# GpSimd in place of VectorE for two elementwise steps of an attention stage: the output bias on the residual tile, and the scale and shift of the turned x

## The chip, the cores and the metric

The kernel runs on one core of one Trainium2 chip. The metric is the device time of one execution in microseconds (us), the median of several runs. The core has a matrix engine (TensorE, PE in the profile; its weight loads are PEld), three engines for elementwise work (VectorE or DVE, ScalarE or ACT, GpSimd or POOL), and SyncE (SP), which here only issues DMAs. Each engine works through its own queue of instructions in the order of the program and waits on semaphores where it needs another's result. DMAs are issued from the queues of SP, ACT and POOL.

## The reference

A transformer-like block on x of shape (8, 512, 1024), float32, in four stages, each with its own layer norm:

```python
x = x + attn_a(_layernorm(x))   # 32 heads of 32, softmax, then ctx @ ow + ob
x = x + ffn(_layernorm(x))      # dense 1024x1024, rows and tokens gated by clusters
x = x + attn_b(_layernorm(x))   # 4 heads of 256, causal sigmoid attention
x = x + ffn(_layernorm(x))
```

The change is in the first line alone. Its layer norm is `(x - m) / sqrt(v + eps)`; its last step is

```python
qkv = x @ attn_qkvw + attn_qkvb
...
return ctx @ attn_ow + attn_ob
```

so that the residual tile gets x + attn_ob + ctx @ attn_ow.

## The kernel before

The 4096 tokens are 8 batches of 512, and 32 tiles of 128 tokens (`NTILE`). The 32 heads are 8 groups of four (`GH`), so the first stage has 64 units: unit n is group g = n % 8 of batch b = n // 8. The first stage takes the span up to about 2530 us; the two dense stages and the sigmoid attention follow.

A unit (the long loop over `n` in `softmax_attention`) has four rounds i = 0 to 3. In a round TensorE computes the scores of unit n+1 by rows (`rows_step`: 16 matmuls, L905, into the one buffer `sc` in PSUM), VectorE takes the negated row maxima from them (L906, out `nmax`), TensorE computes the scores of unit n again by keys into the same buffer `sc` (`keys_step`, L934 and L937), and ScalarE takes the exponential (L939, out `pT`). Between these stand pieces of other work for TensorE, dealt out by `filler`: the projections of unit n+2 (L578, `qk` and `v`), and the output products of the batch before. The one buffer makes a ring: L934 cannot begin before L906 has read `sc`.

The exponentials of the four key tiles are added up: the first two by GpSimd in two halves (L948 in `sum_step`), the third and the fourth by VectorE (L950). The sum ends in the denominators (L973, `normalize`).

When a unit's four maxima are there, `split_max` (called at the end of the unit, for unit n+1) cuts them into three bfloat16 parts with five small VectorE instructions in a row, L912 to L916, on 128 x 16 elements; L913 and L915 are subtractions of two tiles in SBUF. In the first round of the next unit, between its L906 and its L934, TensorE turns these parts (`turn_max`, out `tpm`, line L578 by its helper `product`) for use by L934.

The normalised and turned x of batch b+1 is prepared while batch b runs (`norm_tasks(b + 1)`). x arrives already turned from DRAM (`turned`, L535, tile `xT`); the mean and the root of each token are computed from the straight x (`stats`, `root`, `shift`), sent to DRAM as two rows (`send`, L550) and read back to all partitions (`spread`, L554, tile `rows`). `apply(k, j)` then multiplies a quarter of `xT` (128 x 1024 elements) by the roots (k = 0) or adds the shifts (k = 1) in place, line L558. There are 8 such instructions a batch, for batches 1 to 7: 56. `norm_tasks` lists them for the groups after the one with `spread`: idle, idle and three of them, idle, idle and three more, idle, idle and the last two. These lists go into the deque `side`, which is dealt out over the five calls of `between` in a unit. The Strassen-like sums of the quarters of `xT` (`left_tasks`, L991 and L1377) follow in group 6, and the products of the next batch read those.

The output projection runs over pairs of tiles (`out_pair`), two pairs a batch. `load(m)` brings x's tile into `r` (L766), `bias(m)` adds the broadcast bias `ob_s` in place (L769, 128 x 1024 elements), and `done(k)` adds the products as they end (L788). Of a pair, `bias(0)` is put behind the last product of the pair before, `bias(1)` ahead of the fourth of the seven products; the fourth is the first to add into `r[1]`. `leave(m)` writes the finished tile to DRAM from GpSimd's queue (L816). There are 32 bias instructions; in the last pair the tile is named `spare`, and the lists of the last two pairs run alone, behind the last unit.

GpSimd has, besides L948, the roots (`rstd`, L249, a power on 128 x 1 to 128 x 4 elements) and its DMA issues.

## Time and profile before

| | |
|---|---|
| runs | 3715.86 us median of 3 (3714.45 to 3716.66) |
| span of the profiled execution | 3715.1 us |
| VectorE busy | 2539.7 us, 68% of the span |
| ScalarE busy | 927.8 us, 25% |
| GpSimd busy | 594.9 us, 16% |
| TensorE clock granted | 0.999 of full speed |
| L906 row maxima, VectorE | 256 of 2.289 us each |
| L950 sums, VectorE | 128 of 2.281 us each |
| L249 roots `ln_rstd`, GpSimd | 64 of 0.586 us each |
| L816 write of `r`, issued by GpSimd | 30 of 512 KB, 4.5 us to landing |

A row of the profile names line, engine, operation, what is written from what (`out<-in`, buffer numbers left out), shapes, how many, the busy time in us, the mean of one in ns, and the idle time of the engine just before them with what ended it. A timeline row begins with the start in us and the time taken. The 40 digits in "busy tenths" are shares of equal slices of the span. In lists of waits the last number is the longest single wait.

### The profile page before, as it was taken

The page shows a single profiled execution, that of the slowest core. Times are in us where ns is not written, and L with a number is a line of the kernel's source. Part 1 is how long each engine was busy: PE and PEld are TensorE (multiplying, and loading weights), DVE is VectorE, ACT ScalarE, POOL GpSimd, SP SyncE. Part 2 cuts the span into 40 slices and gives each one's busy share as a digit, 9 for nine tenths or more (in the row PEclk, how much of TensorE's full clock was granted, in tenths as well). Part 3 has the DMA queues.
Part 4 walks back from the last instruction along what each step waited for, and adds up shares of the span by engine and source line. Part 5 has one row for each costly group of instructions (what it writes and reads, how often), then busy time and mean ns, then how long its engine had stood idle before and what let it go on. Part 6 is the DMA issues. An engine that isn't in the chain of part 4 may idle for free.

```text
span 3715.1 us, 76365 instructions
## 1 busy us (share of the span) xinstructions
PE 3677.4 (99%) x32792; PEld 1876.7 (51%) x32792; DVE 2539.7 (68%) x3497; ACT 927.8 (25%) x1017; POOL 594.9 (16%) x574
## 2 busy tenths in 40 slices
PE   8999999999999999999999999999999999999999
PEld 4444544544545455445445445444444467774444
DVE  4777676767667677766767767666788845556656
ACT  1222222222222222222222222222111144430000
POOL 1222111111111111111111111111000044530000
PEclk9999999999999999999999999999999999999999
DMA  5335444645655555465465454347566767763332
GB/s 184 113 122 179 142 143 147 192 138 157 185 153 150 159 162 163 133 198 152 139 182 159 143 150 124 122 156 244 158 180 179 184 186 234 222 220 127 133 132 98
DMA packets 728641, 598.55 MB, mean 161 GB/s; under 512 B 322152, under 2 KB 574064, under 8 KB 728304
## 3 DMA queue, kind: packets, MB, share of 16 engines
q1 hardware_dynamic: 701072, 496.40, 46.6%
q0 software_dynamic: 22912, 81.54, 5.7%
q10 hardware_dynamic: 4320, 15.73, 1.0%
q8 instruction: 259, 4.24, 0.5%
q14 instruction: 78, 0.64, 0.0%
HBM read 459.30 MB, written 134.25 MB: 160 GB/s over the span
## 4 chain that ended last, share of the span: by engine, by line
PE 95%; DVE 3%; DMA 1%; issue 1%; ACT 0%; POOL 0%; SPq 0%; DVEq 0%; ACTq 0%; POOLq 0%
PE mm L578 42%; PE dense L1285 20%; PE sc L905 7%; PE av L961 6%; PE sc L937 6%; PE csc L1347 4%; PE o L1366 4%; PE sc L934 2%; PE logitsT L339 1%; PE den L973 1%; PE tp L291 1%; DVE nmax L906 1%; DVE sum L950 1%; PE tpm L578 0%; DVE s L1377 0%
## 5 line engine op out<-in xcount | busy, mean ns | idle before, releaser
L906 DVE TENSOR_REDUCE nmax<-sc 128x4 f32<-128x2048 f32 x256 | 586.0, 2289 | 295.3 <-PE sc L905 295.2
L939 ACT ACTIVATE pT<-sc 128x2048 f32<-128x2048 f32 x256 | 480.8, 1878 | 1122.3 <-PE sc L937 1122.3
L948 POOL TENSOR_TENSOR sum<-pT,pT 128x1024 f32<-128x1024 f32 x128 | 309.4, 2438 | 750.0 <-ACT pT L939 678.1
L578 PE MATMUL mm<-xT,w 128*64 128x256 f32 (+1 forms) x3736 | 428.1, 383 | 0.0
L578 PEld LDWEIGHTS mm<-xT,w 128*64 128x64 f32 (+1 forms) x3736 | 241.5, 135 | 204.1 <-issue 54.3
L578 PE MATMUL mm<-s,w 128*32 128x256 f32 (+1 forms) x3672 | 321.2, 381 | 1.2 <-DVE qk L158 1.2
L950 DVE TENSOR_TENSOR sum<-sum,pT 128x2048 f32<-128x2048 f32 x128 | 292.0, 2281 | 0.9 <-ACT pT L939 0.9
L905 PE MATMUL sc<-qk,qk 32*64 32x512 f32 x4096 | 285.1, 613 | 0.5 <-ACT pT L939 0.4
L156 DVE TENSOR_TENSOR u<-dense,u 128x512 f32<-128x512 f32 x223 | 148.0, 685 | 184.7 <-PE dense L1285 169.3
L578 PEld LDWEIGHTS mm<-s,w 128*32 128x32 f32 (+1 forms) x3672 | 180.4, 122 | 180.4 <-issue 68.9
L937 PE MATMUL sc<-qk,qk 32*128 32x512 f32 x2048 | 263.7, 589 | 0.0
L578 PE MATMUL mm<-ow,ctxT 128*32 128x512 f32 (+2 forms) x1276 | 247.2, 599 | 3.0 <-DMA ow<-o_T 2.8
L961 PE MATMUL av<-pT,v 128*32 128x512 f32 x2048 | 246.4, 598 | 0.2 <-ACT pT L939 0.2
L1285 PE MATMUL dense<-sum,s 128*128 128x512 f32 x512 | 231.8, 593 | 0.0
L578 PEld LDWEIGHTS mm<-w,xT 128*64 128x64 f32 (+1 forms) x3888 | 197.5, 133 | 62.2 <-issue 48.9
L578 PE MATMUL mm<-w,xT 128*64 128x128 f32 (+1 forms) x3888 | 218.1, 274 | 0.0
L158 DVE SCALAR_TENSOR_TENSOR qk<-mm,qkvb_s,qk 128x256 f32<-128x256 f32 x224 | 107.6, 480 | 123.2 <-PE mm L578 119.2
L1285 PE MATMUL dense<-wT_s,dT_b 128*128 128x512 f32 x384 | 171.2, 593 | 0.0
L1285 PE MATMUL dense<-wT_s,dT_a 128*128 128x512 f32 x384 | 171.2, 593 | 0.0
L578 PE MATMUL mm<-ow,c 128*64 128x512 f32 (+2 forms) x864 | 169.9, 596 | 0.2 <-DMA ow<-in_ow 0.2
L578 PE MATMUL mm<-w,s 128*64 128x128 f32 x2688 | 162.5, 274 | 0.0
L578 PEld LDWEIGHTS mm<-w,s 128*64 128x64 f32 x2688 | 148.0, 137 | 22.9 <-issue 22.9
(236 smaller groups left out, 4468.8 us busy)
## 6 DMA issues: line engine op xcount, KB each, us to landing
w<-in_qkvw SPq DMA_DIRECT2D x252, 256.0 KB, 3.0
ow<-o_T SPq DMA_DIRECT2D x240, 256.0 KB, 3.6
w<-qk_T SPq DMA_DIRECT2D x224, 256.0 KB, 2.8
ow<-in_ow SPq DMA_DIRECT2D x180, 256.0 KB, 3.3
w<-v_T SPq DMA_DIRECT2D x112, 256.0 KB, 2.7
x<-in_x SPq DMA_DIRECT2D x32, 512.0 KB, 5.3
dT_a<-xT SPq DMA_DIRECT2D x32, 512.0 KB, 5.7
x_a<-x SPq DMA_DIRECT2D x32, 512.0 KB, 6.5
```

Of the source, the lines that this page charges most:

```text
L156: nc.vector.tensor_tensor(out, acc, other, ALU.add)
L578: nc.tensor.matmul(out[cols], lhsT[:, cols], rhs, **flags)
L905: nc.tensor.matmul(sc[ts(j, P // 2), h, :], st["q"][rows, cols], st["k"][rows, :], start=True, stop=True)
L906: nc.vector.tensor_reduce(st["nmax"][:, qt, :], sc, AX.X, ALU.max, negate=True)
L937: nc.tensor.matmul(sc[:, h, :], st["k"][rows, ts(kt, P)], st["q"][rows, :], start=False, stop=True)
L939: nc.scalar.activation(pT, sc, AF.Exp, scale=SCALE_A)
L948: nc.gpsimd.tensor_tensor(st["sum"][:, h, :], st["pT", 0][:, h, :], st["pT", 1][:, h, :], ALU.add)
L950: nc.vector.tensor_tensor(st["sum"], st["sum"], st["pT", kt], ALU.add)
L961: nc.tensor.matmul(st["av"][rows, :], st["v"][:, kt, rows], pT[:, h, :], start=(kt == 0), stop=(kt == TPB - 1))
L1285: nc.tensor.matmul(st["acc"], st["left"][LEFT[k]][:, c, :], self.w[RIGHT[k]][:, c, :], start=(c == 0), stop=(c == half - 1),)
L1347: nc.tensor.matmul(sc[:, AT_OFF[i] : AT_OFF[i] + n], k[:, c, ts(i, P)], xT[:, c, i * P :], start=(c == 0), stop=(c == 1),)
L1366: nc.tensor.matmul(acc[:, j - jj, :], at[:, start : start + P], self.v[b * TPB + i][:, cols], start=(i == 0), stop=(i == j),)
```

## The change

Two calls move from VectorE's queue to GpSimd's. Operands, shapes, the place in the program and the arithmetic stay as they are.

```diff
         def apply(k, j):
             part, rows = xT[:, ts(j, 2), :], st["all"][:, k, :].unsqueeze(1).to_broadcast([P, 2, S])
-            nc.vector.tensor_tensor(part, part, rows, (ALU.mult, ALU.add)[k])
+            nc.gpsimd.tensor_tensor(part, part, rows, (ALU.mult, ALU.add)[k])
...
         def bias(m):
-            nc.vector.tensor_tensor(r[m], r[m], ob_s, ALU.add)
+            nc.gpsimd.tensor_tensor(r[m], r[m], ob_s, ALU.add)
```

The queues of TensorE, ScalarE and SyncE keep their instructions and their order; where one of them waited for one of these 88 instructions it now waits for GpSimd. VectorE's queue loses the 88. GpSimd's queue gets them at the places that the program's order gives. For the x of each of the batches 3 to 7 that order is:

```
L948 sum x2
L769 r
L558 xT x3
L816 write of r
L948 sum x2
L249 ln_rstd
L558 xT
L948 sum x2
L558 xT
L816 write of r
L769 r
L558 xT
L249 ln_rstd
L558 xT
L948 sum x2
L558 xT
L948 sum x2
L769 r
```

For batch 2 the first group has one L558 instead of three; for batch 1 the groups are three, three and two, each behind a unit's L948.

## The prediction

> **What bounds the kernel now.** I read the page's first part, then the waits of TensorE in the attention stage (83 to 2530 us, where all 88 moved instructions but the last four lie), then the groups of the moved lines, then timelines.

> ```profile
> PE 3677.4 (99%) x32792; PEld 1876.7 (51%) x32792; DVE 2539.7 (68%) x3497; ACT 927.8 (25%) x1017; POOL 594.9 (16%) x574
> ```

> ```profile
> PE sc L934 <- DVE nmax L906: 4.7, 5, 2.3
> PE den L973 <- DVE sum L950: 1.4, 1, 1.4
> PE mm L578 <- DVE qk L158: 1.2, 6, 0.2
> PE tpm L578 <- DVE parts L916: 1.0, 1, 1.0
> ```

> TensorE is busy 99% of the span; in the stage's 2447.0 us it is busy 2435.9, so 11.1 us is all that any relief of other engines could give there. VectorE is late for it a dozen times only. But lateness is near everywhere: the timelines below show how little room VectorE has at one place.

> **The change part by part.** The groups:

> ```profile
> L558 DVE TENSOR_TENSOR xT<-xT,rows 128x1024 f32<-128x1024 f32 x56 | 73.1, 1308 | 0.2
> L769 DVE TENSOR_TENSOR r<-r,ob_s 128x1024 f32<-128x1024 f32 x30 | 36.5, 1216 | 0.0
> L948 POOL TENSOR_TENSOR sum<-pT,pT 128x1024 f32<-128x1024 f32 x128 | 309.4, 2438 | 750.0 <-ACT pT L939 678.1 <-ACT lg_a L350 40.3 <-DVE c L785 31.6
> ```

> *Removed from VectorE:* 73.1 + 36.5 + 2 x 1.2 = 112 us. On TensorE's time I give this 0: none of the waits above follows a moved instruction in one busy run of VectorE; at the 2.3 us wait, VectorE had last sat idle for TensorE behind its two L558. The bounds are 0 and a gain of 11.1 us.

> *Added to GpSimd:* GpSimd does not run these two forms now. The nearest row is L948, same shape, 2.41 us at the median; another add-like form (L1333, 128 x 1024) takes 2.34, and the largest L948 2.89. I take 2.41: 88 x 2.41 = 212 us on an engine that is idle 84% of the span. So the question is only what becomes late.

> *The bias.* L769 waits for its load and for what stands ahead of it on GpSimd. I put each one behind the end of GpSimd's previous instruction in the trace and added 2.41 us. The consumer L788 then still begins 3.2 us later at the tightest place before the last two pairs, mostly 4.2 us (L948 ends at 1234.55, bias to 1237.0, L788 at 1241.3). Cost 0; were GpSimd slower by more than that 3.2 us, each of some 14 such places would hold VectorE. Behind the bias on GpSimd's queue stand L816's writes, put off by up to 0.5 us; the tiles they write are read in the dense stage, and `r` has three buffers.

> In the last two pairs the queue is tight. At 2528.5 the root L249 would run, the bias follow to about 2531.5, and L788, which began at 2529.63, be 1.9 us late; L261 behind it would wait for the second bias, to 2533.9, and ScalarE's L254 start 2.5 us later than at 2531.62. Its 1.24 us end at 2535.3, ahead of the transposes at 2537.07. Cost between 0 and 1.9 us; I take 1.0.

> *The scale and shift.* The quarter is read by L991 and L1377 a unit later: at least 10 us of room. The instructions queued behind L558 on GpSimd (L948, L249, L816) are put off by at most 0.5 us in this placing. What decides is another thing: the two engines already exclude each other in this trace.

> ```profile
> 519.68 4.79 POOL L948 TENSOR_TENSOR sum<-pT,pT 128x1024 f32<-128x1024 f32 x2 [9.27 <-ACT pT L939]
> 523.62 1.93 DVE L558 TENSOR_TENSOR xT<-xT,rows 128x1024 f32<-128x1024 f32 x1
> L394 DVE TENSOR_TENSOR hits_b<-hits_b,some x7: 226/1290/1314, 3131.9 to 3349.7; 128x64 f32<-128x64 f32 x7
> ```

> (Rows with "x7:" give the count, the shortest, median and longest in ns, the first and last start.) L558 begins under L948, which ends at 524.47, and takes 1.93 us instead of 1.22: its last 1.09 us lie behind that end. So do all seven L558 that meet L948, and L394 of only 128 x 64 elements, 1.29 us instead of 0.22, under GpSimd's L1333. Row maxima L906 (one input, in PSUM) run under L948 at their usual 2.29. So a VectorE instruction with two inputs in SBUF waits for the end of the GpSimd instruction. In the one case with two L948 in a row (2362.7 us, L785 of 2.93 instead of 0.69), VectorE ran between the two and the second took 2.89: they take turns.

> Now the place. For batches 3 to 7 three L558 stand together behind a bias on GpSimd's queue and wait for the DMA `rows`:

> ```profile
> L554 SPq DMA_DIRECT2D rows<-rows x7: 343/422/1022, 168.8 to 2030.1; - x7
> DMA to landing us min/median/max: 5.0/5.2/5.5
> 1399.19 0.42 SPq L554 DMA_DIRECT2D rows<-rows  x1
> 1403.84 2.28 DVE L950 TENSOR_TENSOR sum<-sum,pT 128x2048 f32<-128x2048 f32 x1
> 1408.60 0.20 DVE L912 CAST parts<-nmax 128x16 bf16<-128x16 f32 x1
> 1408.83 0.18 DVE L913 TENSOR_TENSOR rest<-nmax,parts 128x16 f32<-128x16 f32 x1
> 1409.28 0.18 DVE L915 TENSOR_TENSOR rest<-rest,parts 128x16 f32<-128x16 f32 x1
> 1409.50 0.20 DVE L916 CAST parts<-rest 128x16 bf16<-128x16 f32 x1
> 1409.59 2.29 DVE L906 TENSOR_REDUCE nmax<-sc 128x4 f32<-128x2048 f32 x1
> ```

> ```profile
> 1408.14 1.11 PE L905 MATMUL sc<-qk,qk 32*64 32x512 f32 x16
> 1410.96 0.39 PE L578 MATMUL tpm<-ident_h,parts 128*64 128x128 bf16 x8
> 1413.01 0.39 PE L934 MATMUL sc<-shift,ones_h 32*128 32x512 bf16 x4
> ```

> `rows` lands at 1404.17, 0.3 us into VectorE's L950, which has two inputs in SBUF and ends at 1406.12. GpSimd's first L558 therefore runs from there to about 1408.4, the second to 1410.85. VectorE comes to L913 at 1408.83: it waits until 1410.85. L914 follows, and L915 asks at 1411.2, when the third L558 has begun; it waits until 1413.3. L916 ends at 1413.6 instead of 1409.70, and L906 at 1415.8 instead of 1411.88. TensorE's `tpm` had 1.26 us of room behind L916, L934 1.13 us behind L906. Both are used up: L934 begins at 1415.85 instead of 1413.01, 2.9 us late on the engine that bounds. The other four batches have the same rows: L554 at 768.44, 1083.65, 1714.60 and 2030.06, landing 5.0 to 5.5 us later, 0.3 to 0.8 us into an L950. For batch 2 (landing 458.39) one L558 ends at 462.5, ahead of L913 at 462.96: nothing. Batch 1's bursts meet no instruction of this kind.

> Bounds of this term: if GpSimd needs over 0.4 us between one L558 and the next, which waits for it, L913 slips through, L915 alone waits until 1411.4, and 0.9 us is paid; if such small instructions are not held at all, 0. If GpSimd's form takes 2.89 us, as the longest L948, each of the two waits grows by 0.5: 3.9 us. I take 2.9, as the held rows are nearest in kind.

> Elsewhere a single L558 touches L261 and L785 at its last 0.1 to 0.3 us, before an L906 with 1.1 us of room; without that room 0.3 us each.

> [...] No run here shows a held L913 or L915 yet.

> *Sum:* 3715.1 (profiled span) + 5 x 2.9 + 1.0 (tail) - 0 = 3730.6. The median of the runs stands 0.76 above that span: 3731 us, 0.4% slower.

> **The rivals.**

> *One turn slips:* L913 gets in between two L558. 5 x 0.9 + 1.0: 3721. For it: only 0.4 us are missing. Against it: instructions of VectorE that wait for each other follow at 0.04 us (L912 to L913), and GpSimd needs ten times that.

> *The lock spares the small ones (not slower):* L913 and L915 stream through under GpSimd. It decides from where their two waits together stay under 1.13 us, the room of L934. Then 0 to 1 us remains: 3716, VectorE 112 us less busy, and no gain, as TensorE had no wait there. For it: no L913 ever met GpSimd in this trace. Against it: L394, and L248 of 128 x 4 elements that took 0.87 instead of 0.16 us under L948.

> *GpSimd is slower at these forms:* `rows` is read twice through a broadcast, which L948 does not do. Each us more costs 2 us in each of the five places, 10 in all, and from 3.2 us more the biases come late too. With 3.8 us an instruction: 3745. Against it: L1333 and L948 lie within 0.1 us.

> *Relief counts:* TensorE's matmul ends are modelled, and VectorE's delays could hide in them. At most 11.1 us: 3705. Against it: the units' lengths repeat from batch to batch with waits of 0.2 us or less.

> **How the numbers follow.** Forecast 58% (own range 3725 to 3738), one turn 11%, spared 14%, slow form 12%, relief 5%. A measurement of this kernel can tell about 0.2%, 7.4 us, from no change. Slower by more: forecast and slow form, 70%. Within: one turn and spared, 25%. Faster: relief, 5%. The range goes from 3714, just below the spared case, to 3740, the forecast with 3.3 us an instruction, and leaves out most of the slow form and the relief.

> **What would show it.** L558 and L769 on GpSimd near 2.4 us; five L913 and five L915 of about 2 us in place of 0.185; five waits of `tpm` or L934 of some 2.9 us together, each after a landing of `rows`; waits of L788 for GpSimd only behind 2528 us. I am wrong if L913 and L915 keep 0.185 us throughout, if the landing moves out of L950's time, or if waits appear in other units.

## The result, and the profile after

The changed kernel took 3735.23 us (median of 4 runs, 3733.58 to 3737.54), the kernel before 3715.36 us beside it (4 runs, 3714.45 to 3716.66): a ratio of 1.0055, 95% interval 1.0043 to 1.0067. It is some 20 us slower, more than the 0.2% that the prediction gave as the least that can be told from no change. The profiled execution after has a span of 3734.0 us, 18.9 more than before.

First the page's row of busy times, after:

```profile
PE 3682.3 (99%) x32792; PEld 1877.1 (50%) x32792; DVE 2463.6 (66%) x3409; ACT 928.0 (25%) x1017; POOL 806.2 (22%) x662
```

VectorE is busy for 76.1 us less and GpSimd for 211.3 us more, and TensorE is as full as it was. (The moved instructions were 112 us of VectorE's time; some of the others now take longer, as the rows below show, and that counts as busy.) Next, TensorE's waits in the attention stage (83 to 2550 us), after:

```profile
PE tpm L578 <- DVE parts L916: 14.9, 6, 2.9
PE sc L934 <- DVE nmax L906: 4.7, 5, 2.3
PE den L973 <- DVE sum L950: 1.4, 1, 1.4
PE mm L578 <- DVE qk L158: 1.2, 6, 0.2
```

Of the four rows that were shown of before, three stand unchanged. Only the row of `tpm` has grown, from one wait of 1.0 us to six waits of 14.9 us in all. Who was late is seen in the rows of single lines, after (count, shortest/median/longest in ns, first and last start, form):

```profile
L558 POOL TENSOR_TENSOR xT<-xT,rows x56: 2330/2362/3840, 192.8 to 2156.8; 128x1024 f32<-128x1024 f32 x56
L912 DVE CAST parts<-nmax x64: 191/194/2250, 68.1 to 2516.3; 128x16 bf16<-128x16 f32 x64
L913 DVE TENSOR_TENSOR rest<-nmax,parts x64: 184/185/2339, 68.4 to 2516.5; 128x16 f32<-128x16 f32 x64
L914 DVE CAST parts<-rest x64: 202/203/2280, 68.6 to 2516.8; 128x16 bf16<-128x16 f32 x64
L915 DVE TENSOR_TENSOR rest<-rest,parts x64: 183/185/189, 68.8 to 2517.0; 128x16 f32<-128x16 f32 x64
```

Three of the small instructions have a longest of about 2.3 us where their median is 0.2; L915 has none. The place, the preparation of batch 5, in the timeline after (start in us, time taken, in brackets the idle time ahead and what ended it):

```profile
1405.74 1.20 SPq L554 DMA_DIRECT2D rows<-rows  x1
1410.44 2.28 DVE L950 TENSOR_TENSOR sum<-sum,pT 128x2048 f32<-128x2048 f32 x1
1411.65 8.03 POOL L558 TENSOR_TENSOR xT<-xT,rows 128x1024 f32<-128x1024 f32 x3 [8.49 <-DMA rows<-rows]
1414.74 1.11 PE L905 MATMUL sc<-qk,qk 32*64 32x512 f32 x16
1415.20 2.24 DVE L912 CAST parts<-nmax 128x16 bf16<-128x16 f32 x1
1417.48 2.24 DVE L913 TENSOR_TENSOR rest<-nmax,parts 128x16 f32<-128x16 f32 x1
1419.75 0.20 DVE L914 CAST parts<-rest 128x16 bf16<-128x16 f32 x1
1419.99 0.18 DVE L915 TENSOR_TENSOR rest<-rest,parts 128x16 f32<-128x16 f32 x1
1420.21 0.20 DVE L916 CAST parts<-rest 128x16 bf16<-128x16 f32 x1
1420.30 2.28 DVE L906 TENSOR_REDUCE nmax<-sc 128x4 f32<-128x2048 f32 x1
1420.47 0.41 PE L578 MATMUL tpm<-ident_h,parts 128*64 128x128 bf16 x8 [2.73 <-DVE parts L916]
1422.64 0.39 PE L934 MATMUL sc<-shift,ones_h 32*128 32x512 bf16 x4
```

Read it from the burst. The three L558 occupy GpSimd from 1411.65 to 1419.68: the first waits for the end of L950 at 1412.72, then three of about 2.3 us follow. L912 comes at 1415.20, just after the second has begun, and ends with it at 1417.44; L913 comes at 1417.48, just after the third has begun, and ends with it at 1419.72. L914, L915 and L916 then run at their usual length. `tpm`, ready to start at 1417.74, waits 2.73 us, and L934 with it. The reduction L906 begins behind the burst, late by the two holds, and has its usual 2.28.

Where the 18.9 us are, from the starts of `tpm`, unit by unit, after minus before:

| part of the span | after minus before, us |
|---|---|
| five units with such a burst (batches 3 to 7) | 2.91 + 3.05 + 2.90 + 2.92 + 2.91 = 14.69 |
| the unit behind the burst, in two of the five places | 1.66 + 1.67 = 3.3 |
| the same unit in the other three | 0.4 together |
| last `tpm` to the end of the span | +1.5 |
| start, up to the first units | -1.2 |
| the rest | 0.2 |

The 3.3 us were not foreseen. TensorE did not wait in those two units; it ran slower. The windows, after (us; busy us and count of PE, PEld, DVE, ACT and POOL; the granted clock; DMA share; GB/s):

```profile
1098.09:1101.50 3.41, 1.06 (x16) 0.81 (x18) 3.34 (x4) 0.77 (x2) 1.78 (x1) 1.00 0.27 77
1101.50:1104.91 3.41, 3.41 (x23) 1.37 (x18) 3.41 (x3) 0.00 (x0) 0.00 (x0) 0.50 0.14 22
1736.39:1739.80 3.41, 0.77 (x14) 0.62 (x16) 3.31 (x5) 0.90 (x3) 1.84 (x1) 1.00 0.26 77
1739.80:1743.21 3.41, 3.41 (x22) 1.67 (x22) 3.41 (x2) 0.27 (x1) 0.00 (x0) 0.50 0.02 5
1418.94:1422.36 3.42, 1.89 (x24) 1.24 (x24) 3.32 (x5) 0.58 (x1) 0.74 (x1) 1.00 0.25 77
1422.36:1425.77 3.41, 3.38 (x36) 1.09 (x36) 2.81 (x3) 1.74 (x1) 0.00 (x0) 1.00 0.22 77
```

After the stalls that end at 1100.4 and about 1739 the clock granted to TensorE was 0.50 for 3.41 us, which costs half of that, 1.7 us; after the stall that ends at 1420.47 it stayed at 1.00.

### The profile page after: what moved, and what is told of

Its sections match the earlier page's. It is cut to its first block, busy times and chain, and to the rows that moved or that the text cites. A ratio compares the mean times of both kernels' runs of the same rounds, so it can differ in the third digit from the quotient of the medians.

```text
span 3734.0 us, 76377 instructions
## 1 busy us (share of the span) xinstructions
PE 3682.3 (99%) x32792; PEld 1877.1 (50%) x32792; DVE 2463.6 (66%) x3409; ACT 928.0 (25%) x1017; POOL 806.2 (22%) x662
## 4 chain that ended last, share of the span: by engine, by line
PE 93%; DVE 4%; DMA 1%; issue 1%; SPq 0%; ACT 0%; POOL 0%; DVEq 0%; ACTq 0%; POOLq 0%
PE mm L578 41%; PE dense L1285 20%; PE sc L905 7%; PE av L961 6%; PE sc L937 6%; PE o L1366 4%; PE csc L1347 4%; PE sc L934 2%; PE logitsT L339 1%; PE den L973 1%; PE tp L291 1%; DVE nmax L906 1%; DVE sum L950 1%; PE tpm L578 0%; DMA cx<-x 0%
## 5 line engine op out<-in xcount | busy, mean ns | idle before, releaser
L906 DVE TENSOR_REDUCE nmax<-sc 128x4 f32<-128x2048 f32 x256 | 586.0, 2289 | 308.2 <-PE sc L905 308.2
L939 ACT ACTIVATE pT<-sc 128x2048 f32<-128x2048 f32 x256 | 480.8, 1878 | 1127.8 <-PE sc L937 1121.7
L948 POOL TENSOR_TENSOR sum<-pT,pT 128x1024 f32<-128x1024 f32 x128 | 309.6, 2441 | 706.2 <-ACT pT L939 634.3
L578 PE MATMUL mm<-xT,w 128*64 128x256 f32 (+1 forms) x3736 | 430.0, 384 | 0.0
L578 PEld LDWEIGHTS mm<-xT,w 128*64 128x64 f32 (+1 forms) x3736 | 241.9, 135 | 204.9 <-issue 58.6
L578 PE MATMUL mm<-s,w 128*32 128x256 f32 (+1 forms) x3672 | 321.2, 381 | 1.2 <-DVE qk L158 1.2
L950 DVE TENSOR_TENSOR sum<-sum,pT 128x2048 f32<-128x2048 f32 x128 | 292.4, 2284 | 0.9 <-ACT pT L939 0.9
L905 PE MATMUL sc<-qk,qk 32*64 32x512 f32 x4096 | 285.1, 613 | 0.5 <-ACT pT L939 0.4
L578 PEld LDWEIGHTS mm<-s,w 128*32 128x32 f32 (+1 forms) x3672 | 180.4, 122 | 180.3 <-issue 68.9
L156 DVE TENSOR_TENSOR u<-dense,u 128x512 f32<-128x512 f32 x223 | 148.0, 685 | 184.9 <-PE dense L1285 169.2
L578 PE MATMUL mm<-ow,ctxT 128*32 128x512 f32 (+2 forms) x1276 | 247.4, 599 | 3.6 <-DMA ow<-o_T 3.1
L578 PEld LDWEIGHTS mm<-w,xT 128*64 128x64 f32 (+1 forms) x3888 | 197.5, 133 | 62.1 <-issue 48.9
L578 PE MATMUL mm<-w,xT 128*64 128x128 f32 (+1 forms) x3888 | 218.1, 274 | 0.0
L158 DVE SCALAR_TENSOR_TENSOR qk<-mm,qkvb_s,qk 128x256 f32<-128x256 f32 x224 | 107.5, 480 | 154.9 <-PE mm L578 152.2
L578 PE MATMUL mm<-ow,c 128*64 128x512 f32 (+2 forms) x864 | 170.2, 596 | 0.5 <-DMA ow<-o_T 0.5
L578 PE MATMUL mm<-w,s 128*64 128x128 f32 x2688 | 162.5, 274 | 0.0
L578 PEld LDWEIGHTS mm<-w,s 128*64 128x64 f32 x2688 | 148.0, 137 | 22.9 <-issue 22.9
```

The lines of the kernel that those rows point to most:

```text
L156: nc.vector.tensor_tensor(out, acc, other, ALU.add)
L578: nc.tensor.matmul(out[cols], lhsT[:, cols], rhs, **flags)
L905: nc.tensor.matmul(sc[ts(j, P // 2), h, :], st["q"][rows, cols], st["k"][rows, :], start=True, stop=True)
L906: nc.vector.tensor_reduce(st["nmax"][:, qt, :], sc, AX.X, ALU.max, negate=True)
L939: nc.scalar.activation(pT, sc, AF.Exp, scale=SCALE_A)
L948: nc.gpsimd.tensor_tensor(st["sum"][:, h, :], st["pT", 0][:, h, :], st["pT", 1][:, h, :], ALU.add)
```

## The experiments

All times are set against the kernel before on the same chip: 3714.17 us (19 runs) for the first four, 3715.19 us (33 runs) for the last four.

**The bias alone moved**

```diff
 def apply(k, j):
-    nc.gpsimd.tensor_tensor(part, part, rows, (ALU.mult, ALU.add)[k])
+    nc.vector.tensor_tensor(part, part, rows, (ALU.mult, ALU.add)[k])
```

(Diffs here are against the changed kernel.)

> Only the bias moves to GpSimd, the scale and shift stay on VectorE. Theory (three L558 together hold the small instructions of split_max): no L912 to L916 is held, all stay near 0.2 us, and only the last two pairs cost something, 1 to 1.5 us: ratio to before 1.0000 to 1.0005. Rival (every two-input instruction on GpSimd costs VectorE and so TensorE its share, wherever it stands): 32 of 88 of the 19.9 us, 7 us, ratio 1.002.

Measured: 3714.48 us, ratio 1.0001 (0.9991 to 1.0010). TensorE's waits in the stage are those of before, none of L912 to L915 is longer than usual (one L916 took 0.29 us instead of 0.20), and the bias shows in one wait of VectorE:

```profile
DVE r L788 <- POOL r L769: 3.0, 1, 3.0
```

It is the wait behind the last unit, 3.0 us long. Thirty-two instructions moved cost nothing that can be measured, which excludes the rival's 7 us.

**The scale and shift alone moved**

```diff
 def bias(m):
-    nc.gpsimd.tensor_tensor(r[m], r[m], ob_s, ALU.add)
+    nc.vector.tensor_tensor(r[m], r[m], ob_s, ALU.add)
```

> Only the scale and shift move, the bias stays on VectorE. Theory: the five waits of tpm of 2.7 to 2.9 us are there as in the changed kernel, with some drops of the granted clock behind them: 14 to 20 us, ratio 1.004 to 1.0055. Rival (every moved instruction pays alike): 56 of 88, 12.7 us, ratio 1.0034.

Measured: 3731.82 us, ratio 1.0052 (1.0035 to 1.0069). The waits of TensorE, in the same part of the span:

```profile
PE tpm L578 <- DVE parts L916: 14.7, 6, 2.8
```

The loss is here, in full as far as the intervals tell. L912 and L913 took 2.24 to 2.26 us each in all five batches.

**All moved but the three that stand together**

```diff
-    nc.gpsimd.tensor_tensor(part, part, rows, (ALU.mult, ALU.add)[k])
+    (nc.gpsimd if 2 * j + k >= 3 else nc.vector).tensor_tensor(part, part, rows, (ALU.mult, ALU.add)[k])
```

> The whole change, but the first three of the eight L558 of each batch stay on VectorE: 67 of 88 instructions are moved, and none of them stands behind the landing of rows. Theory: tpm waits 0 to 1 us in all as before, no drop of the clock behind it, only the tail's 1 to 1.5 us is left: ratio 1.0000 to 1.0005. Rival (all alike): 67 of 88 of 19.9 us, 15 us, ratio 1.004.

Measured: 3716.92 us, ratio 1.0008 (0.9998 to 1.0017). 67 of the 88 instructions run on GpSimd. The cast keeps its length throughout:

```profile
L912 DVE CAST parts<-nmax x64: 191/194/203, 69.1 to 2498.8; 128x16 bf16<-128x16 f32 x64
```

The waits of `tpm` are back at one of 1.0 us, and the units' lengths are those of before.

**Only the three that stand together moved**

```diff
-    nc.gpsimd.tensor_tensor(part, part, rows, (ALU.mult, ALU.add)[k])
+    (nc.gpsimd if 2 * j + k < 3 else nc.vector).tensor_tensor(part, part, rows, (ALU.mult, ALU.add)[k])
...
-    nc.gpsimd.tensor_tensor(r[m], r[m], ob_s, ALU.add)
+    nc.vector.tensor_tensor(r[m], r[m], ob_s, ALU.add)
```

> The reverse: only the first three L558 of each batch are on GpSimd, 21 instructions of 88. Theory: nearly the whole loss is there, five waits of tpm of 2.7 to 2.9 us plus drops of the clock, 14 to 19 us, ratio 1.004 to 1.005. Rival (all alike): 21 of 88, 4.7 us, ratio 1.0013.

Measured: 3731.20 us, ratio 1.0048 (1.0033 to 1.0063), with the waits

```profile
PE tpm L578 <- DVE parts L916: 14.7, 6, 2.8
```

Twenty-one of the 88 instructions bring the loss, and without them it goes: the two runs together show that the burst is the place.

**One of the three moved, then two**

```diff
-    nc.gpsimd.tensor_tensor(part, part, rows, (ALU.mult, ALU.add)[k])
+    (nc.gpsimd if 2 * j + k < 1 else nc.vector).tensor_tensor(part, part, rows, (ALU.mult, ALU.add)[k])
```

In the second kernel the 1 is a 2; in both the bias is on VectorE.

> Only the first L558 of each batch is on GpSimd. Theory (a held instruction waits to the end of the GpSimd instruction under way, and what counts is what is still under way when L912 comes up): the one L558 starts when L950 ends, takes 2.3 us and is over 0.2 us before L912 comes up; nothing is held, no wait of tpm beyond the 1.4 us of before: ratio 0.9995 to 1.0005. Rival (the loss goes with the number of moved instructions in the place): a third of e4's 17 us, ratio 1.0015.

> The first two L558 of each batch are on GpSimd. Theory: one of L912 and L913 is held to the end of the second, 2.2 us, five times; 1.26 us of that is covered by the room that tpm has, so five waits of tpm of 0.8 to 1.0 us, and no drop of the clock behind waits this short: 4 to 5 us, ratio 1.0010 to 1.0015. Rival (loss by the number): two thirds of e4's 17 us, ratio 1.003.

Measured: with one, 3714.12 us, ratio 0.9998 (0.9989 to 1.0007), and nothing is held:

```profile
L912 DVE CAST parts<-nmax x64: 191/194/199, 69.0 to 2499.0; 128x16 bf16<-128x16 f32 x64
```

With two, 3720.71 us, ratio 1.0016 (1.0007 to 1.0025). The same place of the second kernel in its timeline:

```profile
1405.84 2.28 DVE L950 TENSOR_TENSOR sum<-sum,pT 128x2048 f32<-128x2048 f32 x1
1406.92 5.86 POOL L558 TENSOR_TENSOR xT<-xT,rows 128x1024 f32<-128x1024 f32 x2 [12.97 <-DMA rows<-rows]
1410.60 2.24 DVE L912 CAST parts<-nmax 128x16 bf16<-128x16 f32 x1
1412.87 0.18 DVE L913 TENSOR_TENSOR rest<-nmax,parts 128x16 f32<-128x16 f32 x1
1413.81 0.41 PE L578 MATMUL tpm<-ident_h,parts 128*64 128x128 bf16 x8 [0.68 <-DVE parts L916]
```

L912 is held until the second L558 ends at 1412.78, and L913 runs freely, as there is no third. L912 is 2.05 us longer, and `tpm`'s room (1.26 us in the profile of before) covers all but 0.68 us of it; the five units are 0.85 to 0.91 us longer. So each L558 behind the first held exactly one small instruction; the first hold was covered in good part by the room, and the second, in the kernel with three, found none left. No clock drop followed these short waits.

**The rows read back earlier, the whole change otherwise kept**

```diff
-            [root, shift, send, idle, spread],
+            [root, shift, send, spread],
```

This lets `spread` be issued one call of `between` sooner, so that the burst should be over when the small instructions come.

> The whole change of 88 instructions, with the DMA of rows issued one place earlier (an idle place of the list left out), some 10 us before. Theory: the three L558 run before L950 and are over when L912 comes up; no instruction from L912 to L916 is held, no wait of tpm of over 1 us, no drop of the clock behind it; left is the tail's 1 to 1.5 us: ratio 0.9998 to 1.0008. Rival (VectorE and GpSimd share something in proportion to GpSimd's work): 1.0055 as in the changed kernel.

Measured: 3716.94 us, ratio 1.0005 (0.9996 to 1.0014). The time is back, but not by the way expected. The landing of `rows`, and the same place in the timeline:

```profile
DMA to landing us min/median/max: 7.4/8.4/9.6
1398.38 9.17 POOL L558 TENSOR_TENSOR xT<-xT,rows 128x1024 f32<-128x1024 f32 x3 [3.84 <-DMA rows<-rows]
1401.06 4.27 DVE L950 TENSOR_TENSOR sum<-sum,pT 128x2048 f32<-128x2048 f32 x1
1405.92 1.70 DVE L912 CAST parts<-nmax 128x16 bf16<-128x16 f32 x1
1408.59 0.41 PE L578 MATMUL tpm<-ident_h,parts 128*64 128x128 bf16 x8 [0.23 <-DVE parts L916]
```

The transfer took 8.4 us at the median of the three landings that this profile gives, where it took 5.2 before, and ate about half of what the earlier issue had won: in the five units L554 was issued 6.7 to 9.3 us sooner than in the changed kernel, counted from the `tpm` ahead of it, and the burst began only 3.6 to 5.2 us sooner. The burst had begun when L950 came, held it (4.27 us instead of 2.28), and ended at 1407.55, with L912 taking 1.70 us until then (1.3 to 1.7 us in the five batches). `tpm`'s room covers all but 0.23 us of this. Two holds became one short one; why the transfer took longer in that place was not tried.

**The same, and the last two pairs' bias back on VectorE**

```diff
-            [root, shift, send, idle, spread],
+            [root, shift, send, spread],
...
-            nc.gpsimd.tensor_tensor(r[m], r[m], ob_s, ALU.add)
+            (nc.gpsimd if q < 2 * (B - 1) else nc.vector).tensor_tensor(r[m], r[m], ob_s, ALU.add)
```

> As e7, and the bias of the last two pairs (4 of 32) back on VectorE. Theory: the tail's loss goes too, L788 no longer waits 3.0 us for L769 there; TensorE had no wait to win, so ratio 0.9995 to 1.0003. Rival (relief counts once the collision is gone): VectorE 100 us less busy gives a gain of over 0.1%, ratio under 0.999.

Measured: 3715.19 us, ratio 1.0001 (0.9992 to 1.0010). TensorE's wait for `tpm` is that of before (the second row is that of the busy times):

```profile
PE tpm L578 <- DVE parts L916: 1.0, 1, 1.0
PE 3676.2 (99%) x32792; PEld 1875.6 (51%) x32792; DVE 2455.3 (66%) x3413; ACT 927.9 (25%) x1017; POOL 802.2 (22%) x658
```

VectorE's busy time is 2455.3 us, 84 less than before, and the time is the same. L912 is still held, to 0.7 to 1.7 us in the five batches, within `tpm`'s room. It is the purest view of what the relief of VectorE is worth: nothing, within 0.1%. It also means that no version here beats the kernel before; the best of them equal it.

## Why the prediction came out as it did

The forecast was 3731 us, the measurement 3735.23.

*Relief of VectorE, 0 of at most 11.1 us.* It held. TensorE's three other waits did not change after, and with the loss removed (the last experiment) 84 us less on VectorE left the time where it was. The rival that gave 3705 falls.

*GpSimd's price, 2.41 us an instruction.* L558 took 2.36 and L769 2.38 at the median. The broadcast operand cost nothing more here (L948, without one, has 2.41 in the profile before); the slow-form rival falls.

*The burst, 5 x 2.9 = 14.5 us.* Measured: 14.69. The mechanism was right: a landing under L950, three L558 in a row behind it, two waits of about 2.1 us on VectorE ahead of `tpm`, and 1.26 us of room. The step that failed inside it is the naming of the held instructions. The prediction had L913 and L915 wait, because they have two inputs in SBUF, and let L912 through, because it has one. The cast L912 was held, and L913 behind it; in batch 4, where L912 still ran ahead of the second L558, it was L913 and the cast L914. L915 was never held, since by then no L558 was left to hold it. The sum came out alike because in either reading two holds end with the end of the third L558; that is the luck of this chain, in which casts and subtractions alternate. For a chain of casts alone the prediction's reading would have given no loss at all. The trace of before already had a held instruction with one input, L248, which adds a constant to `ln_mvs`; the prediction took it for its size alone:

```profile
153.95 4.76 POOL L948 TENSOR_TENSOR sum<-pT,pT 128x1024 f32<-128x1024 f32 x2 [0.91 <-ACT pT L939]
157.87 0.87 DVE L248 TENSOR_SCALAR ln_rows<-ln_mvs 128x4 f32<-128x4 f32 x1
```

It ends at 158.74, just behind the end of L948 at 158.71, where 0.16 us is its usual length.

In the profile after, L912 took 2.24 us under L558, while 72 of the L906 ran for more than a microsecond beside an L948 or an L558, and none of the 256 took over 2.293 us. The prediction had gone by the count of inputs in SBUF alone.

*One turn slips (3721), and small ones spared (3716).* Neither occurred: GpSimd started the next L558 of a burst within 0.08 us of the last one's end, ahead of the next small instruction of VectorE, and instructions of 128 x 16 elements were held to the last.

*The bias, 0, and the last two pairs, 1.0 us.* The first held: no wait of VectorE for a bias ahead of the last unit. In the last pairs L788 waited 3.0 us instead of 1.9. What that costs is not resolved: from the start of the last `tpm` to the end, without the 1.7 us of a clock drop where there was one, the four profiles with the bias moved there have 1213.2 to 1214.7 us (mean 1213.7), the six without 1212.8 to 1213.7 (mean 1213.3), so some 0.4 us, with ranges that overlap.

*L261 and L785, covered.* They took 1.8 and 2.4 us longer in all (over the 32 L261 that write `ln_shift` and the 15 L785 that write `c` from `ctxT` alone; one L261 behind the last unit has 1.5 us of this), and no wait of TensorE in the stage came of it.

*What was missing.* The sum had no term for the clock. Two of the five stalls were followed by 3.41 us at half clock, 3.3 us together. That is nearly the difference between the span that the sum gave, 3730.6 us, and the 3734.0 us profiled; the smaller differences (0.2 in the bursts, 0.5 in the tail, 0.6 in other units, -1.2 at the start) cancel.

## What to carry to other kernels

GpSimd was idle 84% of the time before, and was still the wrong place for work under which VectorE's small instructions were held (2.24 us in place of 0.19) at the one moment when VectorE had a short chain of them to answer the bound engine: look at when the moved instructions start, which is set here by a DMA's landing, and not at the share of idle time. The moved instructions that stood in a row brought the loss (3731.20 us with the first three L558 of each batch alone, 3716.92 with the other 67 instructions alone), since each behind the first held one link of the chain and only the first hold met the chain's room (0, 0.9 and 2.9 us a unit for one, two and three). Where work is to leave an engine that is not the bound, first ask whether the bound ever waited for it in those stretches; here it hardly had (8.3 us of waits for VectorE in the stage's 2447), and nothing was won.

## What the runs showed of the hardware

In the profile after, a small VectorE instruction with two inputs in SBUF waited for the end of the GpSimd addition or multiplication that was under way (L913, 2.24 us instead of 0.18), and so did some with a single input in SBUF: the cast of 128 x 16 elements from float32 to bfloat16 (L912, 2.24 us instead of 0.19), and, in the profile before, L248 on 128 x 4 elements (0.87 us instead of 0.16), above. Others ran beside GpSimd at their usual length: the row maxima from PSUM (L906, at most 2.293 us), L248 on 128 x 1 elements (0.154 us at 3056.94 in the profile before, under L1333), and L156, which has one input in PSUM and one in SBUF. In the burst shown above, after:

```profile
1413.12 0.43 DVE L156 TENSOR_TENSOR v<-mm,v 128x256 f32<-128x256 f32 x1 [0.39 <-PE mm L578]
```

Its usual length is 0.42 us. So in these profiles the count of inputs alone did not tell which instruction was held; what sets the two L248 apart was not tried.
